# Pacing a convolution branch by counted engine work in a two-layer graph kernel, with block sums and a norm moved between engines

## The chip, the cores and the metric

The kernel runs on one core of one Trainium2 chip. A core has five engines that run their own instruction queues in order: TensorE (PE, matrix products; its weight loads appear as PEld), VectorE (DVE), ScalarE (ACT), GpSimd (POOL) and SyncE (SP, which here only issues DMA transfers). They meet through semaphores. The metric is the device time of one execution in microseconds (us), lower being better. A profile is one execution recorded by the hardware profiler.

## The reference

There are 64 graphs of N = 256 nodes with D = 256 features, `x` (64, 256, 256), and a 0/1 adjacency `adj` of the same shape. All data is fp32. With the parameters as the setup gives them, what is computed is:

```python
# layer 0
h = relu(bn1(conv1d(x^T, w1, width 1)))                  # (64, 256, 256): channels x positions
h = bn2(conv1d(h, w2, width 17, pad 8))
x_conv = relu(h + x^T)^T
s = x @ w_se.T + b_se                                    # 3 coordinates per node
A = exp(-|s_n - s_m|^2) * adj
x_nmp = A @ relu(x @ w_msg.T + b_msg)
gi = concat(x_conv, x_nmp) @ w_ih.T + b_ih
gh = x @ w_hh.T + b_hh
r, z = sigmoid(gi_r + gh_r), sigmoid(gi_z + gh_z)
g = (1 - z) * tanh(gi_n + r * gh_n) + z * x
x = layernorm(x + g)
# layer 1
h = layernorm(x) * gamma + beta
x = layernorm(x + x + relu((adj @ h) @ W_rel + b_rel + h @ W_root))
```

The output is the last `x`. No layer couples two graphs, so the graphs may be worked on in any order.

## The kernel before

A tile has 128 partitions, so one graph of 256 x 256 is two row chunks of 128, shown in the profile as 128x512. The 64 graphs are taken in `NB` = 8 blocks of `BG` = 8. The kernel has two streams of work.

**The convolution branch.** The 17-tap convolution is done for a whole block at once, because a transform over positions turns it into 47 small products with transformed filters, and eight graphs together make the transform's operands long enough. `conv(b)` is a Python generator that emits this branch for block b, one step at a time: for each pair of graphs, transposes of x on TensorE and the width-1 convolution by `w1` (L440 to L462 of the kernel before; its output goes to `HP` by ScalarE); four VectorE operations of 2048 elements that take `HP` into the big buffer `XF`; split trees on VectorE (L105, by the helper `stt`, and L362); the products (L385, `ps_k1`, `ps_k2`, `ps_k3`), whose results a function `take` brings back, one by a ScalarE copy (L400) and two by VectorE; merge trees on VectorE; the addition of x (`xb`, L546); and transposes back (L535) with a relu to `xc`. The products' filters come from DRAM in tiles of 768 KB, for which there are three buffers. A `yield` ends a step. `yield None` asks in addition that whoever drives the generator stop there, so that a result can arrive before it is used.

**The main stages.** One loop turn k carries several graphs at different stages: `gates(k)`, seven block products of a Strassen-like scheme (L656) accumulated into four PSUM banks `ps_a`, `ps_d`, `ps_b`, `ps_c`, each result added to `g` by VectorE or ScalarE, and two additions on GpSimd (L671, L683); `gates_n(k)`; `update(k)`, the gated sum on VectorE, its norm's statistics, a chain of four small GpSimd operations (L729 to L733, with a power at L730), then four normalising activations on ScalarE (L739); `transposes_h(k-1)`, `project(k-1)` and `aggregate(k-1)`, which are layer 1, its last norm again through VectorE statistics (L707, L708), four GpSimd operations and two activations (L792); and for later graphs `factors(k+2)`, `distances(k+2)`, `mask(k+2)` (the attention matrix `AT`), `passing(k+1)` (`nmp`), `messages(k+3)` (`msg`).

The Strassen-like scheme needs sums of blocks of its left operands. `sums(k, name)` makes four additions or subtractions of 128x128 (L637 to L640) for each of `x` (`xT`), `xc` and `nmp`. They run on GpSimd, except those of `xc` for the first graph of a block, which run on VectorE.

**What sets the order.** The kernel is scheduled by hand: each engine's queue holds the instructions in the order in which the program emits them. Between the main stages of a turn stand ten calls of `pump()`. A pump emits steps of `conv(b + 1)` until the emitted share of that branch's estimated cost reaches the share of pumps called so far (`done < total * at / goal`); the estimate counts VectorE's elements and a fixed weight for TensorE's steps. So block b+1's convolution lies among block b's main stages, spread over eight turns. The last block has no convolution beside it. The first block's convolution is emitted at the head, with a list `early` of first main stages between its steps.

All PSUM tiles are of one bank, eight in rotation (`bank`). `msg`, `nmp`, `AT` and `y` have two buffers, `xT` and `adj` four, `w2` three; `g`, `gn`, `h`, `hT`, `hr` and the sums' tiles have one. SyncE's queue issues the loads in the order emitted: `load(k + 3)` (`xT`, from a DRAM copy that the convolution branch writes), `load_adj(k + 2)`, `load_x(k + 1)`, the convolution's `xn` and `xb`, and the filters. ScalarE's queue issues the DRAM copy `xt` and the output.

Of the kernel before, what the change touches and what calls it, by code (L numbers as in the profile page):

```python
# [16 lines left out]
P = 128  # L17
# [14 lines left out]
RING = 10  # L32
HG = 3 * P
# [42 lines left out]

@with_exitstack
def gnn_two_layers(
# [17 lines left out]
    nc = tc.nc  # L96
    const = ctx.enter_context(tc.tile_pool(name="const", bufs=1))
# [6 lines left out]
    def stt(o, in0, s, in1, op0=ALU.mult, op1=ALU.add):  # L104
        nc.vector.scalar_tensor_tensor(o, in0, s, in1, op0=op0, op1=op1)  # L105
# [26 lines left out]
    nc.vector.memset(mhalf, -0.5)  # L132
    ones = const.tile([P, P], F32)
    nc.vector.memset(ones, 1.0)
# [7 lines left out]
    def batch_norms():  # L142
        for i in range(2):
# [3 lines left out]
            nc.vector.tensor_scalar(sh, v_, EPS, None, ALU.add)  # L147
            nc.gpsimd.tensor_tensor(sc, sh, mhalf[:, :C], ALU.pow)
            nc.vector.tensor_mul(sc, sc, g_)
            nc.vector.tensor_mul(sh, m_, sc)  # L150
            nc.vector.tensor_sub(sh, b_, sh)
# [3 lines left out]
    def along_rows(pool):  # L155

        for i, v in enumerate((bn_scale[1], bn_shift[1])):
            ps = bank("ps_row")
            for c in range(C):
                dg = pool.tile([P, P], F32, tag="dg", name="dg", bufs=4)  # L160
                nc.vector.tensor_scalar(dg, ident, v[:, c:c + 1], None, ALU.mult)
                nc.tensor.matmul(ps[:, c * P:(c + 1) * P], ones, dg, start=True, stop=True)
# [6 lines left out]
    def filters(pool):  # L169
# [18 lines left out]
        def scaled(i, starts):  # L188
# [4 lines left out]
            nc.vector.tensor_mul(  # L193
# [5 lines left out]
        def turned(ws, n):  # L199
            ps = bank("ps_tT")  # L200
            for b in range(n):
                nc.tensor.transpose(ps[:TAPS * OB, b * P:(b + 1) * P], ws[:, b].rearrange("p k o -> p (k o)"), ident)
# [11 lines left out]
        for i, (piece, starts) in enumerate(groups):  # L214
# [7 lines left out]
            for a, o in enumerate(starts):  # L222
                ps = bank("ps_w")
                nc.tensor.matmul(ps[:, :NM * OB], TT[i][:, a, :], tap_sb, start=True, stop=True)
# [67 lines left out]
    def merge(re, im, size, phis, scales, tmp, new):  # L292
# [5 lines left out]
        for base, t in ((re, t_re), (im, t_im)):  # L298
            a, b = halves(base, n, size, False), halves(base, n, size, True)
            tt = temps(t, n, h)  # L300
            if same:
                nc.vector.tensor_sub(tt, a, b)
                yield cost(n * h)
                nc.vector.tensor_add(a, a, b)
# [55 lines left out]
    def butterflies(pairs):  # L360
        for o, a, b, n, add in pairs:
            (nc.vector.tensor_add if add else nc.vector.tensor_sub)(sl(o, n), sl(a, n), sl(b, n))  # L362
# [20 lines left out]
    def product(ps, slot, w, m):  # L383
        for c in range(C):
            nc.tensor.matmul(ps, X[:, slot, c * P:(c + 1) * P], w(m, c), start=(c == 0), stop=(c == C - 1))  # L385

    def products(b, first, sums):
# [10 lines left out]
        def take():  # L398
            k1 = sl(sums, 2).rearrange("p s e -> p (s e)")
            nc.scalar.copy(k1, p1)  # L400
            nc.vector.tensor_sub(sl(re, 2).rearrange("p s e -> p (s e)"), k1, p3)  # L401
            nc.vector.tensor_add(sl(im, 2).rearrange("p s e -> p (s e)"), k1, p2)
        return take

    def last_products(b):
# [10 lines left out]
        def take():  # L416
            nc.scalar.copy(X[:, S2 + 6, :], p1[:, :D])
            nc.scalar.copy(X[:, U + 1, :], p3[:, D:])
            nc.vector.tensor_sub(X[:, U + 2, :], X[:, S2 + 6, :], p2[:, :D])
            nc.vector.tensor_add(X[:, U + 3, :], X[:, S2 + 6, :], p1[:, D:])  # L420

            nc.vector.tensor_add(X[:, U, :], p3[:, :D], bn2_row[:, 1, :])
# [597 lines left out]
```

## Time and profile before

Three runs: 2352.86, 2353.28 and 2354.74 us; the median is 2353.28 us.

| | |
|---|---|
| the profiled execution's own time | 2354.49 us |
| its span (first to last instruction) | 2352.7 us |
| TensorE (PE) busy | 2159.4 us, 92% |
| VectorE (DVE) busy | 1845.6 us, 78% |
| GpSimd (POOL) busy | 971.1 us, 41% |
| ScalarE (ACT) busy | 877.3 us, 37% |
| memory traffic | 226.76 MB, mean 96 GB/s |
| a transfer of one w2 tile (768 KB), issue to landing | 4.9 us |
| a transfer of `xT` (256 KB), issue to landing | 3.9 us |

Block times, taken between TensorE's first gate products of blocks: 188.6 us of head before the first turn, then 279.1, 280.9, 278.0, 278.6, 278.8, 280.7 and 280.2 us for seven blocks that carry a convolution, and 207.8 us for the last block with its tail.

Shares of the span are averages over parts with different limits, so the table alone doesn't say what bounds a turn. In lines that list groups, the first number after the bar is busy time in us, then the mean of one in ns, then the idle time of that engine just before, and what released it. In lines of waits, `DVE g L691 <- PE ps_c L656: 3.8, 2, 2.1` reads: VectorE's line L691, working on `g`, waited for TensorE's `ps_c`, 3.8 us in total, twice, 2.1 at most. L105 is the helper `stt` that all scalar_tensor_tensor operations go through.

### The profile page before, as it was taken

How to read it: one execution, taken by the hardware profiler on the slowest of the kernel's cores; microseconds unless marked ns; L12 is line 12 of the kernel's file. 1: busy time of each engine (PE TensorE's matmuls, PEld its weight loads, DVE VectorE, ACT ScalarE, POOL GpSimd, SP SyncE). 2: the span in 40 equal slices, each digit the busy share in tenths (PEclk: the TensorE clock that was granted, in tenths of full speed). 3: DMA queues.
4: the chain of work that ended last, by engine and by line, in shares of the span. 5: the costliest groups of instructions: out<-in, count | busy, mean ns of one | idle time of the engine just before them, and what ended most of it. 6: DMA issues, size and time to landing. Idle time of an engine off the chain costs nothing.

```text
span 2352.7 us, 25793 instructions
## 1 busy us (share of the span) xinstructions
PE 2159.4 (92%) x8390; PEld 1482.5 (63%) x8390; DVE 1845.6 (78%) x3500; ACT 877.3 (37%) x1809; POOL 971.1 (41%) x1480
## 2 busy tenths in 40 slices
PE   7878899999999999998999999999999999999997
PEld 4565576656666566665676666665666666666664
DVE  3994999759896799949998499975989679895454
ACT  4514322443235432353224432244323533235443
POOL 1003643536334452535435264353533545254442
PEclk9989999999999999999999999999999999999998
DMA  5543152223412243232332225222341214321110
GB/s 161 171 149 117 58 170 63 81 91 110 145 58 83 74 148 112 67 108 76 118 106 90 81 68 170 63 81 94 116 135 63 84 69 148 112 66 52 42 35 18
DMA packets 213939, 226.76 MB, mean 96 GB/s; under 512 B 22327, under 2 KB 205614, under 8 KB 213806
## 3 DMA queue, kind: packets, MB, share of 16 engines
q1 hardware_dynamic: 191248, 191.14, 25.9%
q10 hardware_dynamic: 22558, 33.99, 3.9%
q8 instruction: 67, 1.10, 0.2%
q14 instruction: 66, 0.54, 0.1%
HBM read 179.22 MB, written 45.88 MB: 96 GB/s over the span
## 4 chain that ended last, share of the span: by engine, by line
DVE 44%; PE 42%; issue 6%; POOL 3%; DMA 3%; ACT 2%; SPq 0%; ACTq 0%; DVEq 0%; POOLq 0%
DVE XF L105 16%; PE ps_k L385 7%; PE ps_c L656 5%; PE ps_a L656 5%; PE ps_c L456 4%; PE ps_out L764 4%; PE ps_b L656 3%; DVE XF L362 3%; PE ps_n L700 3%; DVE x L105 3%; DVE bst L707 3%; PE ps_nmp L627 3%; DVE XF L466 2%; PE ps_out L776 2%; PE ps_d L656 2%
## 5 line engine op out<-in xcount | busy, mean ns | idle before, releaser
L105 DVE SCALAR_TENSOR_TENSOR XF<-XF 128x512 f32<-128x512 f32 (+2 forms) x800 | 595.8, 773 | 6.5
L385 PE MATMUL ps_k<-w,XF 128*128 128x256 f32 x1316 | 307.9, 388 | 43.1 <-DVE g L686 21.3
L385 PEld LDWEIGHTS ps_k<-w,XF 128*128 128x128 f32 x1316 | 248.4, 192 | 98.5 <-DVE g L686 26.9
L764 PE MATMUL ps_out<-wrr,hT 128*128 128x512 f32 x512 | 256.3, 648 | 56.2 <-ACT hT L753 56.2
L729 POOL TENSOR_TENSOR q<-mv,eps 128x4 f32<-128x4 f32 x64 | 31.3, 489 | 537.5 <-DVE mv L708 293.9
L764 PEld LDWEIGHTS ps_out<-wrr,hT 128*128 128x128 f32 x512 | 103.2, 206 | 178.5 <-issue 96.6
L594 ACT ACTIVATE msg<-msg 128x512 f32<-128x512 f32 x64 | 40.4, 631 | 359.0 <-DVE msg L588 344.8
L691 DVE TENSOR_TENSOR g<-g,ps_c 128x384 f32<-128x384 f32 x64 | 35.1, 549 | 174.6 <-PE ps_c L656 174.6
L683 POOL TENSOR_TENSOR g<-g 128x384 f32<-128x384 f32 x64 | 77.7, 1214 | 228.0 <-DVE g L681 219.3
L584 PE MATMUL ps_msg<-wms,xT 128*128 128x260 f32 x512 | 134.5, 403 | 8.2 <-DVE XF L401 4.8
L362 DVE TENSOR_TENSOR XF<-XF 128x512 f32<-128x512 f32 (+3 forms) x128 | 135.0, 1080 | 1.8
L456 PE MATMUL ps_c<-xTc,w 128*128 128x512 f32 x256 | 118.1, 604 | 11.4 <-ACT xTc L448 11.4
L627 PE MATMUL ps_nmp<-AT,msg 128*128 128x256 f32 x512 | 122.9, 384 | 1.3 <-DVE AT L620 1.3
L776 PE MATMUL ps_out<-hr,adj 128*128 128x256 f32 x512 | 121.9, 380 | 0.1
L584 PEld LDWEIGHTS ps_msg<-wms,xT 128*128 128x128 f32 x512 | 94.5, 194 | 42.1 <-issue 17.0
L700 PE MATMUL ps_n<-wn,xT 128*128 128x256 f32 x512 | 121.0, 379 | 0.0
L656 PE MATMUL ps_b<-wg,nmpsum 128*128 128x384 f32 x256 | 106.0, 496 | 16.1 <-ACT g L675 14.4
L792 ACT ACTIVATE y<-y,sh,q 128x256 f32<-128x256 f32 x128 | 69.9, 594 | 134.6 <-POOL sh L789 133.9
L700 PEld LDWEIGHTS ps_n<-wn,xT 128*128 128x128 f32 x512 | 97.3, 190 | 26.9
L688 ACT ACTIVATE g<-g 128x512 f32<-128x512 f32 x64 | 40.3, 630 | 197.0 <-DVE g L686 197.0
L776 PEld LDWEIGHTS ps_out<-hr,adj 128*128 128x128 f32 x512 | 96.4, 190 | 15.9 <-ACT hr L765 1.6
L786 POOL TENSOR_SCALAR q<-mv 128x2 f32<-128x2 f32 x64 | 29.2, 457 | 186.1 <-DVE mv L708 186.1
(154 smaller groups left out, 4894.5 us busy)
## 6 DMA issues: line engine op xcount, KB each, us to landing
w<-w2m SPq DMA_DIRECT2D x105, 768.0 KB, 4.9
xn<-in_x_dram SPq DMA_DIRECT2D x32, 512.0 KB, 4.5
xt<-xTc ACTq DMA_DIRECT2D x32, 512.0 KB, 4.3
xT<-xt SPq DMA_DIRECT2D x64, 256.0 KB, 3.9
adj<-in_adjT_dram SPq DMA_DIRECT2D x64, 256.0 KB, 2.7
x<-in_x_dram SPq DMA_DIRECT2D x64, 256.0 KB, 2.8
xb<-in_x_dram SPq DMA_DIRECT2D x32, 512.0 KB, 3.7
out_dram<-y ACTq DMA_DIRECT2D x64, 256.0 KB, 2.2
```

The lines of the kernel that those rows point to most:

```text
L105: nc.vector.scalar_tensor_tensor(o, in0, s, in1, op0=op0, op1=op1)
L362: (nc.vector.tensor_add if add else nc.vector.tensor_sub)(sl(o, n), sl(a, n), sl(b, n))
L385: nc.tensor.matmul(ps, X[:, slot, c * P:(c + 1) * P], w(m, c), start=(c == 0), stop=(c == C - 1))
L456: nc.tensor.matmul(ps, w1[:, c, o * P:(o + 1) * P], xTc[:, c, :], start=(c == 0), stop=(c == C - 1))
L584: nc.tensor.matmul(ps[:, :D + 4], XT[k][:, c, m * P:(m + 1) * P], wms[:, c, :], start=(c == 0), stop=(c == C - 1))
L627: nc.tensor.matmul(ps[:, d * N:(d + 1) * N], MSG[k][:, m, d * P:(d + 1) * P], AT[k][:, m, :], start=(m == 0), stop=(m == C - 1))
L656: nc.tensor.matmul(ps[:, :w.shape[-1]], LEFT[k, name][i], w, start=start and j == 0, stop=j == 2, skip_group_check=not start)
L683: nc.gpsimd.tensor_add(g11, g11, g01)
L700: nc.tensor.matmul(ps[:, n * D:(n + 1) * D], XT[k][:, c, n * P:(n + 1) * P], wn[:, c, :], start=(c == 0), stop=(c == C - 1))
L707: nc.vector.bn_stats(st, src)
L764: nc.tensor.matmul(ps, hT[:, c, n * P:(n + 1) * P], wrr[:, c, :], start=(c == 0), stop=(c == C - 1))
L776: nc.tensor.matmul(po, ADJ[k][:, m, n * P:(n + 1) * P], hr[:, m, :], start=False, stop=(m == C - 1), skip_group_check=True)
```

## The change

1. **Pacing.** VectorE's and TensorE's calls go through wrappers (`ve`, `te`, class `Timed`) that count, at emission, an estimate of each engine's work in a `Clock`: TensorE n x 4/2400 us for a product with n columns, 0.107 for a transpose; VectorE 0.07 + 0.00105 n us. `pump()` emits convolution steps until VectorE's count is `LEAD` = 3.5 us ahead of TensorE's, or the generator yields None. Outside of pumps VectorE's count is first raised to TensorE's (`follows`). The share of an estimated cost is gone; a pump no longer has a quota.
2. **Main stages.** `load(k + 3)` moves from the middle of the turn to its start. `mask` moves from a turn's end (for k + 2) to after the second gate step of the next turn (for k + 1), and `mask(1)` goes from `early`. `messages(k + 3)` moves from after `update`'s second step to before `passing(k + 1)`. The sums of `x` move from before the loads to after `passing(k + 1)`, those of `xc` to after `project`, those of `nmp` to after `distances`. There are still ten pumps a turn, at slightly other places.
3. **Block sums.** All of `sums` runs on VectorE: 184 groups of four small operations move from GpSimd, 736 in all; the other eight groups were on VectorE already.
4. **Last norm.** In `aggregate`, the two bn_stats and two bn_aggr a graph go. The operation y = max(y, 0) + x is split in two halves, each with an accumulated row sum (`total`). GpSimd turns the sum into minus the mean; two ScalarE Square activations with that as bias accumulate the squared deviations, writing their elementwise result into `hr`, which is free by then; three GpSimd operations make scale and shift; the two final activations stay. `aggregate` has four steps instead of three, which are called from more places.

Reused names: `ve` and `te` replace `nc.vector` and `nc.tensor` in the rest of the kernel without other effect; those lines are left out here.

```diff
...
 NB = B // BG
 RING = 10
+LEAD = 3.5
 HG = 3 * P
 PI = math.pi
...
     a = th - PI / 2 if q else th
     return math.tan(a), math.cos(a), q
+class Clock:
+    def __init__(self):
+        self.pe = self.dve = 0.0
+        self.follows = True
+    def tensor(self, name, n):
+        self.pe += 0.107 if name == "transpose" else n * 4 / 2400
+    def vector(self, name, n):
+        if self.follows:
+            self.dve = max(self.dve, self.pe)
+        self.dve += 0.07 + n * 1.05e-3
+class Timed:
+    def __init__(self, engine, spend):
+        self.engine, self.spend = engine, spend
+    def __getattr__(self, name):
+        op = getattr(self.engine, name)
+        def call(o, *args, **kwargs):
+            self.spend(name, math.prod(o.shape[1:]))
+            return op(o, *args, **kwargs)
+        return call
...
 ):
     nc = tc.nc
+    clock = Clock()
+    ve, te = Timed(nc.vector, clock.vector), Timed(nc.tensor, clock.tensor)
     const = ctx.enter_context(tc.tile_pool(name="const", bufs=1))
     conv_pool = ctx.enter_context(tc.tile_pool(name="conv", bufs=2))
...
-    def blocks(src, s1, s2, s3, s4, eng):
+    def blocks(src, s1, s2, s3, s4):
         a11, a12, a21, a22 = (src[:, c, n * P:(n + 1) * P] for n in range(C) for c in range(C))
-        eng.tensor_add(s1, a21, a22)
-        eng.tensor_sub(s2, s1, a11)
-        eng.tensor_sub(s3, a11, a21)
-        eng.tensor_sub(s4, a12, s2)
+        ve.tensor_add(s1, a21, a22)
+        ve.tensor_sub(s2, s1, a11)
+        ve.tensor_sub(s3, a11, a21)
+        ve.tensor_sub(s4, a12, s2)
         return a11, a12, s4, a22, s1, s2, s3
-    def sums(k, name, eng=None):
+    def sums(k, name):
         if name == "x":
             src = XT[k]
...
             t = work.tile([P, 3, P], F32, name=name + "sum", bufs=1)
             s3 = src[:, 0, P:]
-        LEFT[k, name] = blocks(src, t[:, 0, :], t[:, 1, :], s3, t[:, 2, :], eng or nc.gpsimd)
+        LEFT[k, name] = blocks(src, t[:, 0, :], t[:, 1, :], s3, t[:, 2, :])
     def block_product(k, i, ps, start):
...
                                  skip_group_check=True)
-            nc.vector.tensor_add(y[:, n, :], po, brel)
-        yield
-        stt(y, y, 0.0, X1[k], op0=ALU.max, op1=ALU.add)
-        mv = work.tile([P, C, 2], F32, tag="mv", name="mv3", bufs=4)
+            ve.tensor_add(y[:, n, :], po, brel)
+        yield
+        total = work.tile([P, C], F32, tag="q3", name="sum3", bufs=4)
         for n in range(C):
-            stats(mv, n, y[:, n, :])
-        q = work.tile([P, C], F32, tag="q3", name="q3", bufs=4)
+            ve.scalar_tensor_tensor(y[:, n, :], y[:, n, :], 0.0, X1[k][:, n, :], op0=ALU.max, op1=ALU.add,
+                                    accum_out=total[:, n:n + 1])
+        nc.gpsimd.tensor_scalar(total, total, -1.0 / D, None, ALU.mult)
+        yield
+        var = work.tile([P, C], F32, tag="v3", name="v3", bufs=4)
+        for n in range(C):
+            nc.scalar.activation(hr[:, n, :], y[:, n, :], AF.Square, bias=total[:, n:n + 1], accum_out=var[:, n:n + 1])
         sh = work.tile([P, C], F32, tag="sh", name="sh3", bufs=4)
-        nc.gpsimd.tensor_scalar(q, mv[:, :, 1], EPS / 4, None, ALU.add)
-        nc.gpsimd.tensor_tensor(q, q, mhalf[:, :C], ALU.pow)
-        nc.gpsimd.tensor_mul(sh, mv[:, :, 0], q)
-        nc.gpsimd.tensor_scalar(sh, sh, -1.0, None, ALU.mult)
+        nc.gpsimd.tensor_scalar(var, var, 1.0 / D, EPS / 4, ALU.mult, ALU.add)
+        nc.gpsimd.tensor_tensor(var, var, mhalf[:, :C], ALU.pow)
+        nc.gpsimd.tensor_mul(sh, total, var)
         yield
         for n in range(C):
-            nc.scalar.activation(y[:, n, :], y[:, n, :], AF.Identity, bias=sh[:, n:n + 1], scale=q[:, n:n + 1])
+            nc.scalar.activation(y[:, n, :], y[:, n, :], AF.Identity, bias=sh[:, n:n + 1], scale=var[:, n:n + 1])
         nc.scalar.dma_start(out=out[k].rearrange("(c p) d -> p c d", p=P), in_=y)
         yield
...
                 nc.gpsimd.tensor_sub(w[:, i], w[:, j], w[:, l])
     early = [lambda: messages(0), lambda: messages(1), lambda: factors(0), lambda: distances(0), lambda: mask(0),
-             lambda: factors(1), lambda: distances(1), lambda: mask(1), lambda: passing(0), lambda: messages(2),
+             lambda: factors(1), lambda: distances(1), lambda: passing(0), lambda: messages(2),
              lambda: sums(0, "x"), lambda: weight_sums((6, 2, 4), (4, 4, 0)), lambda: sums(0, "nmp"),
              lambda: weight_sums((5, 2, 4), (3, 1, 5))]
...
     for f in early:
         f()
-    sums(0, "xc", nc.vector)
-    POINTS = 10
+    sums(0, "xc")
+    clock.pe = clock.dve = 0.0
     y_left = up_left = None
     for b in range(NB):
         coming = conv(b + 1) if b + 1 < NB else iter(())
-        done, at, goal = 0.0, 0, BG * POINTS - 6
         def pump():
-            nonlocal done, at
-            at += 1
-            while done < total * at / goal:
-                t = next(coming, 1e9)
-                if t is None:
-                    break
-                done += t
+            clock.follows = False
+            while clock.dve < clock.pe + LEAD and next(coming, None) is not None:
+                pass
+            clock.follows = True
         for k in range(b * BG, (b + 1) * BG):
             ga, up = gates(k), update(k)
+            load(k + 3)
             step(ga)
+            step(y_left)
             step(up_left)
+            pump()
+            step(ga)
+            if k + 1 < B:
+                mask(k + 1)
+            step(y_left)
             pump()
             step(ga)
             step(y_left)
             pump()
-            step(ga)
-            pump()
             if k + 2 < B:
                 factors(k + 2)
             step(ga)
-            if k + 1 < B:
-                sums(k + 1, "x")
-                if (k + 1) % BG:
-                    sums(k + 1, "xc")
-            load(k + 3)
             load_adj(k + 2)
             load_x(k + 1)
...
             if k > 0:
                 transposes_h(k - 1)
+            if k + 3 < B:
+                messages(k + 3)
             pump()
             if k + 1 < B:
                 passing(k + 1)
-                sums(k + 1, "nmp")
+                sums(k + 1, "x")
             step(ga)
             gates_n(k)
...
             if k > 0:
                 project(k - 1)
+            if k + 1 < B and (k + 1) % BG:
+                sums(k + 1, "xc")
             step(up)
             pump()
             if k + 2 < B:
                 distances(k + 2)
+            if k + 1 < B:
+                sums(k + 1, "nmp")
+            pump()
             step(up)
             pump()
-            if k + 3 < B:
-                messages(k + 3)
-            pump()
-            if k + 2 < B:
-                mask(k + 2)
             agg = None
             if k > 0:
                 agg = aggregate(k - 1)
-            step(agg)
             step(agg)
             pump()
...
             pass
         if b + 1 < NB:
-            sums((b + 1) * BG, "xc", nc.vector)
+            sums((b + 1) * BG, "xc")
+    step(y_left)
     step(up_left)
+    step(y_left)
     step(y_left)
     transposes_h(B - 1)
     project(B - 1)
     agg = aggregate(B - 1)
-    for _ in range(3):
+    for _ in range(4):
         step(agg)
...
```

## The prediction, made before the changed kernel was run

> **What bounds the kernel now.** I read the page's slices first. TensorE is busy 92% of the span and VectorE 78%, so an average says TensorE. The chain that ended last says otherwise:
>
> ```profile
> DVE 44%; PE 42%; issue 6%; POOL 3%; DMA 3%; ACT 2%; SPq 0%; ACTq 0%; DVEq 0%; POOLq 0%
> ```
>
> The two take turns. So I cut one block of eight graphs, a typical one of 279 to 281 us, at the instruction that begins each turn. The table of windows (microseconds; then busy time and count of TensorE, weight loads, VectorE, ScalarE, GpSimd; then clock and DMA) shows six turns of the block, its other two, and a turn of the last block, where no convolution runs:
>
> ```profile
> 1079.30:1285.00 205.70, 187.44 (x741) 131.75 (x740) 194.82 (x363) 65.34 (x136) 102.13 (x138) 0.99 0.31 100
> 1285.00:1358.30 73.30, 71.86 (x282) 46.73 (x281) 35.64 (x73) 38.45 (x74) 22.39 (x45) 1.00 0.27 90
> 2169.00:2192.90 23.90, 23.90 (x94) 16.30 (x93) 12.33 (x32) 10.15 (x21) 10.26 (x23) 1.00 0.14 45
> ```
>
> For six turns VectorE is the bound (194.82 of 205.70; 205.70 - 187.44 is TensorE idle). For two, TensorE is (71.86 of 73.30), while VectorE has 38 us free. A main turn alone is 23.9 us of TensorE. VectorE's waits in the six turns are few:
>
> ```profile
> DVE g L691 <- PE ps_c L656: 3.8, 2, 2.1
> DVE gn L703 <- PE ps_n L700: 2.3, 2, 1.2
> DVE g L686 <- POOL g L683: 0.9, 1, 0.9
> DVE gn L105 <- ACT g L692: 0.2, 1, 0.2
> ```
>
> That is 7.2 us. TensorE's waits there (to ScalarE and VectorE) cost nothing while VectorE is the bound. What VectorE's time is made of shows in the groups of the same six turns, by shape:
>
> ```profile
> L105 DVE SCALAR_TENSOR_TENSOR XF<-XF 128x512 f32<-128x512 f32 x56 | 44.6, 821 | 0.6
> L105 DVE SCALAR_TENSOR_TENSOR y<-y,x 128x512 f32<-128x512 f32 x6 | 4.2, 692 | 0.2
> L683 POOL TENSOR_TENSOR g<-g 128x384 f32<-128x384 f32 x6 | 8.0, 1328 | 24.1 <-DVE g L681 24.1
> L640 POOL TENSOR_TENSOR nmpsum<-nmp,nmpsum 128x128 f32<-128x128 f32 x6 | 5.6, 930 | 0.0
> ```
>
> The same operation on 128x512 is 692 ns in one place and 821 on average in the convolution; single ones reach 888 where GpSimd is in a two-input operation. GpSimd pays too: a sum is 930 here and 454 to 458 in the quiet last block. I fitted VectorE's pitch, start to start, where GpSimd is idle: 0.066 + 0.00104 n us (0.33 for 256 elements, 0.60 for 512, 2.20 for 2048), 0.12 more if it reads the result just before. Priced so, the six turns hold 174.3 us; the remainder is 21.3 over price while GpSimd works (12.5 beside the block sums L637 to L640, 7.2 beside L671 and L683, 1.6 beside small ones), 2.4 other excess, and 7.3 gaps: 205.3 of 205.7.
>
> [...] Here a quiet sum is 454 against VectorE's 290. [...] but starts follow each other closer:
>
> ```profile
> 1030.83 0.26 DVE L637 TENSOR_TENSOR xcsum<-xc 128x128 f32<-128x128 f32 x1
> 1031.12 0.29 DVE L638 TENSOR_TENSOR xcsum<-xcsum,xc 128x128 f32<-128x128 f32 x1
> 1031.33 0.30 DVE L639 TENSOR_TENSOR xc<-xc 128x128 f32<-128x128 f32 x1
> 1031.56 0.28 DVE L640 TENSOR_TENSOR xcsum<-xc,xcsum 128x128 f32<-128x128 f32 x1
> 1031.76 0.54 DVE L670 TENSOR_TENSOR g<-g,ps_d 128x384 f32<-128x384 f32 x1
> ```
>
> Four sums on VectorE take 1031.76 - 1030.83 = 0.93 us.
>
> **The change part by part**, per block, with the instruction order that the changed program is built with.
>
> *Sums.* Three kinds a turn move to VectorE, 18 groups of four in the six turns, less one that was there: at 0.93 us about +16, and the 12.5 us of interference beside them go. That L671 and L683 stay keeps 7.2.
>
> *Last norm.* VectorE loses bn_stats and bn_aggr twice a turn (0.446 and 0.099 us apart), 1.09, and the 128x512 y operation (0.73) becomes two of 256 with an accumulated sum (about 0.78): about -1.0 a turn. Together main work on VectorE goes from 10.9 to 12.5 us a turn. ScalarE gains two Squares of 128x256 with accumulation; no row shows them. The nearest is L739, 598 ns; lower bound that[...]. I take 0.6, since ScalarE is busy 65 of 205.7 us, hence hidden; in the tail, where nothing hides it, it counts. GpSimd's small operations are as many as before.
>
> *Pacing.* It moves convolution steps. Summed by the built order, a turn's work is (TensorE / VectorE, turns 0 to 7): before 41.4/22.0, 24/24.5, 24/21.9, 44.8/41.4, 39.6/35.1, 28.4/28.8, 24.9/23.0, 26.7/13.1; after 41.4/15.7, 24/24.7, 24/25.0, 24/21.4, 50/51.9, 38.8/39.5, 24/26.9, 27.5/16.9. Turns 1 to 6 of VectorE: 174.7 to 189.4, that is six times 1.6 plus 4.9 of convolution work brought in (three 2.2-us operations from turn 0 enter, 1.1 of xb additions leave to turn 7, the rest rounding).
>
> *Six VectorE-bound turns after:* 189.4 + 2.5 other + 7.2 + 1.6 = 200.7. The four waits above mostly go, as VectorE holds conv work ahead of each. New ones come: the take of a product at the start of turn 5, whose VectorE subtraction waits for a ScalarE copy that stands behind four normalisations (2.2 + 1.1 us after the GpSimd chain), 3.0; a ScalarE relu of msg ahead of such a copy in turns 4 and 5, 0.6 and 1.2; g at turn 4, 0.3; margin 0.5. Sum 206.3, against 205.7: nothing gained.
>
> *Two TensorE-bound turns after:* work is 41.4 + 27.5 = 68.9 against 68.1, but 73.3 were used: 5.2 is VectorE's backlog and waits of TensorE for it. With the front-loaded operations gone from turn 0, I expect 0.6 to 1.7 of waits, of which 1.2 is new (the relu of msg(k+3) holds ScalarE while xTc copies queue behind it): 69.5 to 70.6, a gain of 2.7 to 3.8.
>
> *DMA.* The same transfers. load(k+3) now stands first on SP's queue in a turn; xT lands 3.9 us after issue and is needed some 13 us later, when messages(k+3) runs. It passes the adj and x loads, which have a turn or more to spare. Weights w take 4.9 us and are fetched three tiles ahead. I price it at nothing; a late w would cost up to 4.9 once.
>
> *Mask* moves from the turn's end to after the second gate step; passing(k+1) needs it half a turn later. Free; otherwise 0.6 a turn on VectorE's lag.
>
> *Ends.* The last graph's norm has no cover: two Squares for two stats, one more GpSimd operation (0.46), hT copies behind them: +3.4; the head has its first sums on VectorE, +1.5.
>
> Sum per block -0.6 + (2.7 to 3.8) = -2.1 to -3.2; seven blocks -15 to -22, ends +4.9: -10 to -17. The profiled execution was 2354.49 us (span 2352.7), so 2337 to 2344; the median of the runs shown is 1.2 lower, 2353.28. I forecast **2340**.
>
> **Rivals.**
> *Nothing to measure (13%).* The bounded turns stay full and TensorE's two turns keep 3.1 us of waits (68.9 + 3.1 = 72.0); the gain of 1.3 less 0.6, 0.7 a block, is cancelled by the ends: 2349 to 2358. For it: the convolution's front in turn 0 (transposes, then products by w1) gives VectorE nothing to do, so that its 38 free us can't be filled and the pacing does not balance what it counts. That is the case of a change that doesn't do what it says.
>
> *Large gain (17%).* Takes don't wait, since the copy's chain starts early enough (-5.1), and two-thirds of the remaining interference goes with calmer GpSimd timing (-3): six turns 198.2, two 69.2, a block 267.4 against 279.0: seven times -11.6, ends +4.9: about 2278. For it: GpSimd loses 12 of its 14 large operations a turn; against it: L671 and L683 directly follow VectorE work, so they still run beside its next operation.
>
> *Slower (32%).* messages(k+3) now stands before passing(k+1), and msg has two buffers. The VectorE addition that writes msg(k+3) therefore waits until TensorE has read msg(k+1) in passing(k+1), which in TensorE's queue comes after the message products; ScalarE's relu waits for the addition. Behind the addition stand all of VectorE's convolution operations, behind the relu ScalarE's copies of products, and TensorE waits for those. TensorE between the two has 1.7 us of nmp products and whatever the pump puts there, up to a product of 5.2. It decides where VectorE lags TensorE by less than about 4.5 us, the wait then being the difference. By the built order I get a lag of 4.2 to 4.9 at that place. At 3 us the wait is 1.5 a turn in 42 turns, +63: 2403; at 3.5 it is +42: 2382. So this side is centred on 2390.
>
> **Numbers.** Forecast 38%, its own range 2328 to 2348; with the large gain, faster is 0.55. Within 0.2% (4.7 us, about what a measurement of this kernel tells from no change) 0.13, slower 0.32. Of the 2 in 10 left out about half lies at each end: 2288 to 2390.
>
> **What would show it.** Right: L637 to L640 on VectorE at 0.21 to 0.29 pitch; XF operations of 128x512 near 740 ns; DVE busy about 200 in the six turns, waits on ScalarE's k1 copy of 3 us once a block; two turns of 70. Wrong if: VectorE waits for TensorE at msg L588 of before (the slower case), the six turns lie off 206 by over 4, or the y chain through two more engines delays hT, and TensorE with it, every turn.

## The result: slower by 1.8%

The changed kernel's median is 2396.05 us (2393.95 to 2399.2) against 2354.01 us of the kernel before in the same series. The ratio is 1.0178 (95% interval 1.0161 to 1.0196): 42 us lost, where the forecast was 13 us gained. The profiled execution has a span of 2392.4 us, 39.7 more than before.

Cut at the same instruction of VectorE (the sum of `ps_d` into `g`) as in the prediction, the table of windows of the changed kernel shows the six turns, the other two, and a turn of the last block. The columns are as before.

```profile
1090.60:1305.00 214.40, 197.18 (x756) 139.96 (x755) 195.67 (x429) 71.32 (x159) 48.99 (x65) 0.97 0.29 95
1305.00:1376.50 71.50, 67.99 (x267) 44.86 (x266) 34.74 (x90) 41.34 (x82) 14.03 (x27) 0.95 0.28 96
2206.40:2230.30 23.90, 23.90 (x93) 16.30 (x92) 14.83 (x43) 10.99 (x25) 5.76 (x11) 1.00 0.15 45
```

The two turns improved by 1.8 us. The six turns grew from 205.70 to 214.40. VectorE's busy time there is nearly the same as before (195.67 against 194.82), so nearly all of the added time is idle time. Its waits in those six turns:

```profile
DVE g L106 <- ACT g L710: 5.4, 3, 2.6
DVE XF L106 <- ACT XF L435: 4.3, 3, 3.0
DVE g L106 <- POOL g L718: 3.0, 3, 1.3
DVE msg L106 <- PE ps_nmp L106: 2.1, 1, 2.1
DVE g L106 <- PE ps_d L106: 1.4, 2, 1.1
```

All of VectorE's operations are on L106 now, since they go through one wrapper; tiles tell them apart. L710 is the ScalarE copy of `ps_b` into `g` (L675 before), L435 the copy of a product (L400 before), L718 the GpSimd addition (L683 before). Of the five only the third stood in the list of before, with 0.9 us; the first two are 9.7 us of waiting for ScalarE. The timeline shows one wait for the `ps_b` copy. The columns are start, duration, engine, line, operation and tiles:

```profile
1402.76 0.18 DVE L106 BATCH_NORM_AGGREGATE mv<-bst 128x2 f32<-128x6 f32 x1
...
1403.02 0.20 POOL L764 TENSOR_TENSOR q<-mv,eps 128x4 f32<-128x4 f32 x1 [12.81 <-DVE mv L106]
1403.30 1.04 POOL L765 TENSOR_TENSOR q<-q,mhalf 128x4 f32<-128x4 f32 x1
1404.42 0.37 POOL L767 TENSOR_TENSOR sh<-mv,q 128x4 f32<-128x4 f32 x1
1404.88 1.09 POOL L768 TENSOR_SCALAR sh<-sh 128x4 f32<-128x4 f32 x1
...
1406.00 1.09 ACT L774 ACTIVATE h<-x,sh,q 128x256 f32<-128x256 f32 x2 [4.41 <-POOL sh L768]
1407.00 1.08 ACT L774 ACTIVATE x<-x,sh,q 128x256 f32<-128x256 f32 x2
1407.98 0.46 ACT L710 COPY g<-ps_b 128x384 f32<-128x384 f32 x1
...
1408.47 0.56 DVE L106 TENSOR_TENSOR g<-g,ps_c 128x384 f32<-128x384 f32 x1 [2.59 <-ACT g L710]
```

Read it as a loop. VectorE ends the statistics of `update(k-1)` at 1402.94. GpSimd turns them into scale and shift until 1405.97. ScalarE then runs four normalising activations. Behind them in its queue stands the copy of `ps_b` for the next graph's gates, whose product had been ready since 1402. VectorE needs the copied `g` for the sum of `ps_c`, and stands for 2.59 us, with its convolution work queued behind that sum. The least time from statistics to that sum is about 4.6 us (2.0 to 2.2 on GpSimd at its shortest, 1.98 of activations, 0.5 of copy). I measured this distance in each turn, as a mean over five blocks. In the kernel before it is 4.6 in one turn of eight, and 7 to 16 in the others. In the changed kernel it is between 4.7 and 6.1 in seven turns of eight. In four of these turns VectorE waits for the copy, and its own work in the stretch is 1.8 to 3.9 us. Three things of before no longer lie in it: the additions of `messages`, the product that `mask` makes (in this turn it starts at 1408.94, after the sum), and the last norm's statistics.

Blocks take 283.1 to 285.9 us now, 278.0 to 280.9 before: +33.6 us over seven. The head adds 4.0 (192.6 against 188.6) and the last block 2.1 (209.9 against 207.8), which sums to the 39.7.

### The profile page after: what moved, and what is told of

Its sections match the earlier page's. It is cut to its first block, busy times and chain, and to the rows that moved or that the text cites. A ratio compares the mean times of both kernels' runs of the same rounds, so it can differ in the third digit from the quotient of the medians.

```text
span 2392.4 us, 26243 instructions
## 1 busy us (share of the span) xinstructions
PE 2173.5 (91%) x8390; PEld 1508.2 (63%) x8390; DVE 1869.8 (78%) x4172; ACT 946.0 (40%) x2065; POOL 506.9 (21%) x744
## 5 line engine op out<-in xcount | busy, mean ns | idle before, releaser
L106 DVE SCALAR_TENSOR_TENSOR XF<-XF 128x512 f32<-128x512 f32 (+2 forms) x800 | 521.9, 688 | 6.8
L106 DVE TENSOR_TENSOR XF<-XF 128x256 f32<-128x256 f32 (+3 forms) x480 | 357.5, 764 | 43.9 <-ACT XF L494 36.3
L106 PE MATMUL ps_k<-w,XF 128*128 128x256 f32 x1316 | 295.1, 380 | 2.9 <-DVE msg L106 1.5
L106 PEld LDWEIGHTS ps_k<-w,XF 128*128 128x128 f32 x1316 | 250.8, 191 | 51.4 <-issue 4.3
L106 PE MATMUL ps_out<-wrr,hT 128*128 128x512 f32 x512 | 232.2, 596 | 4.6 <-ACT hT L788 4.6
L106 PE MATMUL ps_b<-wg,nmpsum 128*128 128x384 f32 x256 | 115.5, 535 | 107.7 <-ACT g L710 85.5
L106 PEld LDWEIGHTS ps_out<-wrr,hT 128*128 128x128 f32 x512 | 97.4, 192 | 103.4 <-issue 89.2
L106 PE MATMUL ps_nmp<-AT,msg 128*128 128x256 f32 x512 | 130.5, 400 | 25.2 <-DVE g L106 22.5
L774 ACT ACTIVATE h<-x,sh,q 128x256 f32<-128x256 f32 x128 | 69.8, 593 | 200.9 <-POOL sh L768 200.9
L631 POOL TENSOR_SCALAR st<-ns 128x4 f32<-128x4 f32 x64 | 25.4, 397 | 580.8 <-DVE sq L106 357.8
L106 DVE TENSOR_TENSOR g<-g,ps_c 128x384 f32<-128x384 f32 x128 | 70.4, 550 | 90.6 <-ACT g L710 63.9
L106 PE MATMUL ps_msg<-wms,xT 128*128 128x260 f32 x512 | 127.8, 393 | 3.9 <-DMA adj<-in_adjT_dram 3.5
L106 PEld LDWEIGHTS ps_b<-wg,nmpsum 128*128 128x128 f32 x256 | 44.2, 198 | 137.6 <-ACT g L710 93.6
L106 PE MATMUL ps_out<-hr,adj 128*128 128x256 f32 x512 | 128.1, 392 | 1.0 <-ACT hr L800 0.9
L106 PEld LDWEIGHTS ps_nmp<-AT,msg 128*128 128x128 f32 x512 | 99.8, 199 | 43.4 <-DVE g L106 25.4
L106 PE MATMUL ps_c<-xTc,w 128*128 128x512 f32 x256 | 118.2, 604 | 8.6 <-ACT xTc L483 8.6
L718 POOL TENSOR_TENSOR g<-g 128x384 f32<-128x384 f32 x64 | 84.5, 1320 | 183.9 <-DVE g L106 183.2
L106 DVE TENSOR_TENSOR msg<-ps_msg,bmsg 128x256 f32<-128x256 f32 x128 | 52.5, 416 | 88.7 <-PE ps_nmp L106 88.7
L106 PE MATMUL ps_n<-wn,xT 128*128 128x256 f32 x512 | 120.9, 379 | 0.0
L106 PE MATMUL ps_c<-wg,nmp 128*128 128x384 f32 x256 | 110.0, 513 | 9.1 <-DVE y L106 9.1
L831 ACT ACTIVATE y<-y,sh,v 128x256 f32<-128x256 f32 x128 | 69.9, 593 | 121.1 <-POOL sh L828 118.3
```

What stands on the lines that cost most here:

```text
L106: return op(o, *args, **kwargs)
L631: nc.gpsimd.tensor_scalar(twice[:, :, :, 3], ns.unsqueeze(2).to_broadcast([P, C, 2]), 0.5, None, ALU.mult)
L718: nc.gpsimd.tensor_add(g11, g11, g01)
L774: nc.scalar.activation(dst[:, n, :], w[:, n, :], AF.Identity, bias=sh[:, i, n:n + 1], scale=q[:, i, n:n + 1])
L831: nc.scalar.activation(y[:, n, :], y[:, n, :], AF.Identity, bias=sh[:, n:n + 1], scale=var[:, n:n + 1])
```

## Experiments

Three theories were on the table. N: the loop through ScalarE's queue is the cause. V: VectorE is full in the six turns, and waits are only where slack shows. M: the prediction's slower rival, two buffers of `msg`. Edits are to the changed kernel unless said otherwise. "Six" and "two" are the two kinds of turns, mean of five blocks (before 206.5 and 72.8, changed 213.7 and 70.4), "idle" is VectorE's idle time in the six, in gaps of over 0.1 us (before 8.1, changed 14.5). I call the loop open in a kernel where VectorE no longer waits for the `ps_b` copy in the six turns, closed where it does as in the changed kernel.

### The copy ahead of the activations

```diff
             step(y_left)
-            step(up_left)
             pump()
             step(ga)
+            step(up_left)
             if k + 1 < B:
                 mask(k + 1)
```

> The four normalising activations of update(k-1) are emitted after the second gate step instead of before it, so ScalarE's copy of ps_b, and at the start of a turn the copy of a product, stand ahead of them. Theory N (those copies wait behind activations that wait for the GpSimd chain, and VectorE waits for the copies: in a block 8.3 us at the ps_b copy and 4.3 us at the product's copy): the two waits fall below 2 us a block, a block from 284 to 272-276, the time to 2312-2340 us. Theory V (the six turns are full of VectorE work, 199 us of it, and a wait only shows where slack is): the waits turn up elsewhere, 2386-2396 us. Theory M (msg waits for nmp): unchanged, 2396 us.

Measured: 2340.34 us, 0.9945 of before (0.9928 to 0.9962). Six 205.4, idle 5.7, two 71.5. One block's six turns of this kernel, in the view of VectorE's waits:

```profile
DVE g L106 <- POOL g L718: 3.0, 3, 1.2
DVE XF L106 <- ACT XF L435: 1.3, 2, 1.1
DVE g L106 <- PE ps_d L106: 1.1, 1, 1.1
DVE msg L106 <- PE ps_nmp L106: 0.4, 1, 0.4
```

The wait for the `ps_b` copy is gone, the product's copy waits 1.3 instead of 4.3, and 56 us come back. No work was removed. By the traces TensorE, VectorE and GpSimd run the changed kernel's instructions in its order; only ScalarE's order differs. N holds, V falls: in the six turns no other wait took their place. In the two turns one did: TensorE's wait for the `ps_b` copy (3.4 us a block) goes, and one of 3.2 us for a ScalarE copy of `lr` comes (`PE ps_xc <- ACT lr`), and these turns take 71.5, not less than 70.4.

### The messages late, and both edits

```diff
-            if k + 3 < B:
-                messages(k + 3)
             pump()
             if k + 1 < B:
                 passing(k + 1)
...
             step(up)
             pump()
+            if k + 3 < B:
+                messages(k + 3)
             agg = None
```

> messages(k+3) goes back behind update's second step, where it stood before, so the addition into msg finds passing(k+1) done. Theory M: VectorE's wait for nmp (10.2 us a block, 6.7 of them in the turn that TensorE bounds and so free) goes, 3.5 us a block, 2371 us. Theory N: the message additions also come between the statistics and the ps_b copy and cover about 1 us of each of four waits, so 2360-2375 us, with the wait for the ps_b copy still 4 us a block. Theory V: 2391-2401 us.

> Both edits at once, activations after the ps_b copy and messages late; each alone had brought the changed kernel to 2340 and 2338 us. Theory N (one loop: statistics on VectorE, GpSimd chain, four activations, ps_b copy, and VectorE's next use of it; either edit opens it): nothing left to gain twice, only what is over of waits in the six turns (product copy 1.3, nmp 1.0 us), 2325-2340 us. Theory of two separate causes: the two gains of 56 us add, 2285-2300 us.

Measured: 2338.41 us (0.9931, 0.9915 to 0.9947) for the messages alone, 2339.51 (0.9937, 0.9918 to 0.9956) for both. The first gained more than any theory gave it: the `ps_b` wait did not shrink, it vanished. TensorE's message products and VectorE's additions now lie between the statistics and the sum of `ps_c`, which come 5.5 us or more apart in every turn. This edit also takes away the wait that M names, and the order on every engine shifts with it, so it is the less clean test of the two. Two edits worth 56 and 58 us alone are worth 57 together. They open the same loop. What is left differs: with the messages late the six turns are 208.2 with idle 7.7, of which 3.3 is a new wait for `ps_d`, and the two turns are 68.5.

### Three buffers of msg

```diff
-        MSG[k] = work.tile([P, C, D], F32, tag="msg", name="msg")
+        MSG[k] = work.tile([P, C, D], F32, tag="msg", name="msg", bufs=3)
...
-        y = work.tile([P, C, D], F32, tag="y", name="y")
+        y = work.tile([P, C, D], F32, tag="y", name="y", bufs=1)
```

> The changed kernel with three buffers of msg (y has one instead of two to make room), so that the addition into msg(k+3) has no wait for passing(k+1); the order is the changed kernel's. The rival of the prediction (two buffers of msg hold VectorE): the wait for nmp, 1.6 us a block in the six turns and 9.4 in the two, goes. If it is also what sets off the waits for the ps_b copy: 2338-2350 us. If it is only its own 1.6 us a block: 2380-2390 us. Theory N: the waits for the ps_b copy stay at 5 us in the six turns, 2380-2396 us.

Measured: 2380.62 us (1.0109, 1.0092 to 1.0126). VectorE's waits in six turns:

```profile
DVE g L106 <- ACT g L710: 5.4, 3, 2.6
DVE XF L106 <- ACT XF L435: 4.2, 3, 3.0
DVE g L106 <- POOL g L718: 3.0, 3, 1.3
DVE g L106 <- PE ps_d L106: 1.1, 1, 1.1
```

The wait for `ps_nmp` is gone as built, the two waits for ScalarE stand within a tenth. (Every engine runs the changed kernel's instructions in its order.) So the rival's mechanism exists and costs 15 us, and is not what the other waits come from.

### Two of four activations ahead of the copy

```diff
             for n in range(C):
                 nc.scalar.activation(dst[:, n, :], ...)
+            if i:
+                yield
...
             step(ga)
+            step(up_left)
             if k + 1 < B:
                 mask(k + 1)
...
```

> Only two of the four normalising activations (those of h) stand ahead of the ps_b copy, the other two follow it. Theory N: each of the four waits of a block shortens by two activations, 1.1 us: the wait for the ps_b copy in the six turns from 5.4 to about 2.2 us a block, for the product's copy from 4.3 to 3.2, in all -5.5 us a block with the seventh turn, 2355-2362 us. Theory of a wait that is set by something else than the activations: 2390-2396 us.

Measured: 2361.36 us (1.0029, 1.0021 to 1.0037). The `ps_b` wait is 2.6 (2.2 expected), the product's copy 3.3 (3.2 expected). Four activations ahead: 2396; two: 2361; none: 2340. The order on the other engines is again the same. The wait follows the length of what stands ahead of the copy.

### A longer lead, with the loop closed and open

```diff
-LEAD = 3.5
+LEAD = 6.0
```

> The pacing's lead is 6.0 us instead of 3.5. Theory N: VectorE holds 2.5 us more of convolution work ahead of each of the four waits of 2 to 3 us for the ps_b copy, which shrink to below 1 us: 2340-2365 us. Theory V: the same VectorE work in the six turns, only earlier, 2390-2400 us. Theory M: a larger lag of VectorE hides its wait for nmp in the six turns, 1.5 us a block, 2385 us.

> The first experiment's order (activations after the ps_b copy) with a lead of 6.0 us. Theory N says that the longer lead hurt the changed kernel (2411 us) because VectorE reaches the norm's statistics later while TensorE's b product is no later, so that five of eight turns, not four, waited on the loop. With the loop open the lead has nothing to hurt: 2330-2345 us. If a longer lead costs by itself, by late product results or full buffers: 2350-2360 us.

Measured: 2411.3 us (1.0239, 1.0219 to 1.026) in the changed kernel, 2333.75 (0.9916, 0.989 to 0.9943) with the copy ahead of the activations. The first refutes my expectation: I had thought that more convolution work queued on VectorE would cover the wait. It is queued in front of the statistics too, so the loop starts later: measured from the end of the `ps_b` product, the statistics end 0.8 to 7.9 us later than in the changed kernel in four of eight turns. Six turns of eight stand at 5.2 us or less, and the `ps_b` wait doubles to 10.3 us. With the loop open the same lead does no harm.

### Block sums back on GpSimd, or moved alone

```diff
-        LEFT[k, name] = blocks(src, t[:, 0, :], t[:, 1, :], s3, t[:, 2, :])
+        LEFT[k, name] = blocks(src, t[:, 0, :], t[:, 1, :], s3, t[:, 2, :], eng or nc.gpsimd)
```

(`blocks` calls its four operations on `eng` again.) In the changed order, then with the copy ahead of the activations; third, the kernel before with `eng` always VectorE:

> All of the change but the block sums, which go back to GpSimd at their new places. Theory V: VectorE's work in six turns falls by 16 us, interference beside the sums returns with 12, and the copies wait as before, but VectorE is no longer full: 2360-2380 us. Theory N: the waits for the copies stay, and a sum's four operations on GpSimd (3 us) are now ahead of the GpSimd chain of the norm, so that it starts later: 2396-2420 us. Theory M: 2396 us.

> The first experiment's order with all block sums back on GpSimd. With the loop open, the prediction's term for the sums stands alone: -15.8 us of VectorE's work and +12.5 of interference in the six turns, -3 us a block: 2315-2335 us. If the sums on GpSimd delay what waits for GpSimd (the norm's chain, the additions to g), or their products: 2345-2365 us.

> The kernel before with nothing changed but the block sums, all on VectorE. By the prediction's sum: in the six turns +15.8 us of work and -12.5 of interference, +3.3 us a block less what was idle there, so 2354-2378 us. If the interference beside the sums costs more than the sums do on VectorE: 2330-2350 us. If VectorE is full and interference is not freed: up to 2460 us.

Measured: 2417.21 us (1.0268, 1.025 to 1.0286); 2339.04 (0.9934, 0.9915 to 0.9954); 2376.51 (1.009, 1.007 to 1.011). In the kernel before, moving the sums costs 21 us: six turns 209.2, +2.7, where the prediction's sum had +3.3. VectorE's time without idle grew by more, 6.8 (the sums take 16.8, and 10.0 of other operations' time goes); idle fell from 8.1 to 3.9. In the open loop it is worth nothing (2339 against 2340), which lies between the two expectations. In the closed loop GpSimd sums make all worse, with idle 28.8 (the `ps_b` copy 8.1, `msg` 4.5, the GpSimd addition 3.8). In two turns the norm's activations start 1.2 and 1.9 us later after the statistics, in another VectorE has 3.0 us less to do while it waits. What each of these costs was not taken apart.

### The last norm, three times

The norm's statistics back on VectorE (`bn_stats`, `bn_aggr`), no Squares: with the copy ahead, then in the changed kernel; third, the kernel before with only the new norm.

```diff
-        total = work.tile([P, C], F32, tag="q3", name="sum3", bufs=4)
-        for n in range(C):
-            ve.scalar_tensor_tensor(y[:, n, :], ..., accum_out=total[:, n:n + 1])
...
+        stt(y, y, 0.0, X1[k], op0=ALU.max, op1=ALU.add)
+        mv = work.tile([P, C, 2], F32, tag="mv", name="mv3", bufs=4)
+        for n in range(C):
+            stats(mv, n, y[:, n, :])
```

> The first experiment's order with the last norm's statistics back on VectorE (bn_stats), without the Squares on ScalarE. By the prediction's term, VectorE has 1.0 us more in each turn, 6 us in the six turns that it bounds, and seven blocks: +42 less what the tail wins back (3), so 2370-2380 us. If ScalarE's Squares cost as much as they free: 2335-2345 us.

> The changed kernel, its loop as it is, with only the last norm's statistics back on VectorE. Theory N: the two bn_stats and bn_aggr add 1.1 us of VectorE work a turn between update's statistics and the use of the ps_b copy, which is inside the loop, where VectorE was waiting anyway: each wait shortens by 1.1 us as in the experiment with two of four activations, and with what the norm gave in the open loop (-23 us) 2335-2355 us. The prediction's term alone (+1.0 us a turn on a full VectorE): 2430-2438 us. If only the open loop gained: about 2396 us.

> The kernel before with only the new last norm, Squares on ScalarE. The prediction's term: VectorE 1.1 us less a turn, 6.6 in the six turns, seven blocks, tail +3: 2310-2330 us. Theory N: VectorE's work saved lies inside the loop of statistics, activations and ps_b copy only where the loop is tight (in the kernel before one turn of eight is at its least time), so a gain of part of that: 2325-2345 us. If the Squares cost on ScalarE what they free, as the open-loop runs hint: 2355-2380 us.

Measured: 2316.94 us (0.9843, 0.9826 to 0.9861); 2340.89 (0.9955, 0.994 to 0.997); 2316.15 (0.9851, 0.983 to 0.9871). Six turns of the last one, which is the kernel before with one part of the change:

```profile
1063.90:1264.30 200.40, 185.38 (x741) 131.78 (x742) 187.61 (x356) 70.29 (x158) 101.21 (x138) 1.00 0.33 104
```

VectorE is busy 7.2 us less than before (187.61 against 194.82) and the six turns are 5.3 us shorter (200.40 against 205.70). The same part in the changed order is a loss of 55 us (2396 against 2341). There the last norm's statistics lie between the loop's start and end. Taking 1.1 us of them away gave VectorE nothing to do earlier; it only waited longer. With them back, one block's six turns have

```profile
DVE XF L106 <- ACT XF L435: 1.7, 2, 1.1
DVE g L106 <- ACT g L710: 1.5, 3, 0.6
```

in place of 4.3 and 5.4.

That the open loop too runs 23 us faster with the old norm I had not expected: by the prediction's term it should have lost, to 2370 to 2380. VectorE pays the 6.0 us in the six turns that the sum says; of it come back 3.7 in convolution operations (two fewer fall into the six turns), 0.9 in the mask and 1.6 of idle time, so the six turns stay at 205, and the two turns shorten from 71.5 to 68.3, with less waiting for `ps_nmp`. The pacing places steps differently, as its count gives a `bn_stats` of six results 0.08 us where the trace has 0.45. That this is why is argued, not shown.

### The old pump in the new order

```diff
             clock.follows = False
-            while clock.dve < clock.pe + LEAD and next(coming, None) is not None:
-                pass
+            nonlocal done, at
+            at += 1
+            while done < total * at / goal:
+                ...
```

Made with the copy ahead of the activations.

> The first experiment's order of main stages, sums and norm with the old pump, which follows the share of an estimated cost. If the count is what makes the order work: VectorE's backlog returns into the two turns that TensorE bounds (+3 us a block) against 4.9 us less convolution work in the six turns that VectorE bounds, and waits where the quota leaves VectorE without work (7 us a block in the kernel before): 2345-2375 us. If the pacing is worth nothing: 2335-2345 us. If the quota is better with the loop open: 2315-2333 us.

Measured: 2366.41 us (1.0048, 1.003 to 1.0067), 26 us slower than with the count. Six turns have idle 10.8, of which 8.9 is VectorE's `msg` waiting for `ps_nmp`. So the prediction's slower rival costs most here, where the quota, as I read it, leaves VectorE too little work just ahead of that addition.

### The two GpSimd additions to g on VectorE

```diff
-        nc.gpsimd.tensor_add(g00, g00, bg[:, 1, :])
+        ve.tensor_add(g00, g00, bg[:, 1, :])
...
-        nc.gpsimd.tensor_add(g11, g11, g01)
+        ve.tensor_add(g11, g11, g01)
```

Made in the 2317 us kernel (copy ahead, old norm).

> The fastest kernel so far (2317 us: activations after the copy, norm's statistics on VectorE) with the two additions to g moved from GpSimd to VectorE. VectorE gains 2 x 0.47 us a turn, 5.6 in the six turns; of interference beside these two up to 7.2 us and of waits for the GpSimd addition 2.9 us go, all in all -4.5 us a block: 2285-2300 us. If the remaining excess of VectorE isn't interference: 2330-2345 us.

Measured: 2411.55 us (1.0253, 1.0232 to 1.0274), a clear miss. VectorE's time without idle in the six turns went from 200.9 to 201.7 only, though 5.9 us of additions came in. That is not interference gone. Eight of the convolution's operations left the six turns for the two, as one block of each kernel shows (the 2317 us kernel first):

```profile
L106 DVE SCALAR_TENSOR_TENSOR XF<-XF 128x512 f32<-128x512 f32 x55 | 36.7, 701 | 0.5
L106 DVE SCALAR_TENSOR_TENSOR XF<-XF 128x512 f32<-128x512 f32 x47 | 30.7, 685 | 0.5
```

The eight account for some 5.5 us. Those that stayed became only 16 ns shorter each, 0.8 us in all, where up to 7.2 us of interference was expected to go. Idle rose from 4.1 to 11.5 (`msg` for `ps_nmp` 5.0, product's copy 4.6), and the two turns, where VectorE's work grew by 6.7 us, from 68.3 to 74.2. The pump's counts shift with every operation moved, and with them where products and trees land. Which shift did it is open.

## Why the prediction was wrong, and where it was right

*VectorE's work in the six turns: right.* 200.7 us without waits were forecast, 199.2 measured (mean of five blocks). Interference beside the sums went: the convolution's 128x512 operations, 821 ns before and "near 740" forecast, are

```profile
L106 DVE SCALAR_TENSOR_TENSOR XF<-XF 128x512 f32<-128x512 f32 x56 | 38.2, 715 | 0.6
L824 ACT ACTIVATE hr<-y,sum 128x256 f32<-128x256 f32 x12 | 6.0, 503 | 1.7 <-POOL sum L820 1.7
```

The second line is the Square, 0.50 us apart, where 0.6 was taken. Single terms of the sum were off. No group of sums stood on VectorE in these six turns before, so 18 came, not 17; and three additions of `xb` left them, not one. The terms of single parts, tested on the kernel before, held in time: the sums +2.7 a block against +3.3, the new norm -37 us in all against -1.0 x 42 + 3 = -39. In part that is luck, since VectorE's work moved by more (+6.8 and -8.1 in the six turns) and its idle time took up the difference (3.9 and 10.3, for 8.1 before).

*The two turns: the number right, by luck.* They take 70.4, against 69.5 to 70.6. The forecast was 68.9 of TensorE's work and 0.6 to 1.7 of waits. TensorE is busy 66.0 there and waits 4.3 (mean of five blocks), most of it in this line (one block):

```profile
PE ps_b L106 <- ACT g L710: 3.0, 1, 3.0
```

It is the `ps_b` copy again, for which TensorE waits as well.

*The waits: wrong, and this is the step that failed.* "The four waits above mostly go, as VectorE holds conv work ahead of each. New ones come", with 5.6 us in all. The measured sum is 14.5 (mean of five blocks): the `ps_b` copy 5.4 and the GpSimd addition 3.0 were not in it, unless the 0.3 for `g` in one turn stood for the latter; the product's copy was 4.3 instead of 3.0, and `msg`, which the forecast left to its slower rival, 1.6. The chain of the four normalisations behind the GpSimd operations was named, but only for a product's copy at the start of one turn. The `ps_b` copy stands behind the same four activations in every turn. I took VectorE's queued work to cover it, and did not subtract, turn by turn, the VectorE work between statistics and use from the 4.6 us that the loop needs at least. In the changed order, where `messages`, the mask and the last norm's statistics no longer lie between, that work is less than the loop in four turns of eight. Either the messages or the statistics put back end most of the waiting for the copy (2338 and 2341 us); the mask alone was not tried. With the loop open (the copy ahead) the waits are 5.7 and the time is 2340.34, the forecast's 2340. That it meets the forecast so closely is chance: the six turns are 205.4 against 206.3, the two 71.5 against 69.5 to 70.6.

*The ends:* +4.0 at the head against +1.5, +2.1 at the tail against +3.4, of little weight.

*The slower rival: the number right, the mechanism mostly not.* It gave 2382 to 2403 by `msg` waiting for `passing`. That wait is 1.6 us in six turns, and a third buffer wins 15 us of 56. The larger part is the loop. A time that lies in a rival's band does not prove the rival.

*The large gain* needed the product's copy not to wait; it waited more.

*What the change is worth by parts* depends on what it is combined with: the new norm alone gains 37 us in the old order and loses 55 in the new one; the count gains 26 us over the quota in the new order with the loop open; the sums cost 21 us in the old order and nothing in the open new one. Fastest were the kernel before with the new norm (2316 us) and the changed kernel with the copy ahead and the old norm (2317 us). The first with the copy moved as well was not tried.

## What to carry to other kernels

Where queues run in order, write down every loop that leaves an engine and returns to it (here VectorE, GpSimd, ScalarE, VectorE), its least time, and the returning engine's own work between the two ends; when stages are moved, recompute that difference in each turn before counting any work saved. Work saved inside such a loop turned into waiting here (1.1 us a turn of the last norm's statistics, a loss of 55 us in the changed order), and queued work in front of its start made it worse (a lead of 6.0 instead of 3.5 us, 15 us more). In a queue, an operation whose input is ready (here the copy of `ps_b`, worth 56 us) belongs ahead of those that still wait for another engine.

## What the runs showed of the hardware

TensorE's busy time rose from 2159.4 to 2173.5 us with the same 8390 matmuls, and the mean granted clock fell from 0.976 to 0.962; with the loop open it is 0.975. The table of windows over a few us of the changed kernel, in a turn where VectorE's sums of `nmp` are late, shows a stretch at half clock (start and end, length, then busy time of TensorE, its weight loads, VectorE, ScalarE, GpSimd; third from the end the clock):

```profile
1504.60:1506.60 2.00, 1.57 (x6) 0.76 (x4) 1.93 (x7) 0.00 (x0) 0.00 (x0) 1.00 0.00 0
1506.60:1508.60 2.00, 0.00 (x0) 0.00 (x0) 1.97 (x4) 0.00 (x0) 0.00 (x0) 1.00 0.00 0
1508.60:1510.60 2.00, 1.78 (x5) 1.22 (x6) 1.93 (x6) 0.00 (x0) 0.00 (x0) 0.82 0.00 0
1510.60:1512.60 2.00, 0.93 (x2) 0.00 (x0) 1.86 (x7) 0.48 (x1) 0.00 (x0) 0.50 0.00 0
1512.60:1514.60 2.00, 1.56 (x3) 0.95 (x4) 1.87 (x8) 0.00 (x0) 1.61 (x3) 0.50 0.04 8
1514.60:1516.60 2.00, 2.00 (x5) 1.23 (x4) 0.00 (x0) 1.73 (x4) 1.38 (x3) 0.50 0.00 0
1516.60:1518.60 2.00, 2.00 (x10) 1.76 (x9) 1.16 (x2) 2.00 (x7) 0.00 (x0) 0.97 0.00 0
```

TensorE waits 2.7 us, works on, and then has half the clock for 6.83 us (1509.89 to 1516.72), with another wait of 1.5 us in them. In the changed kernel's clock records 32 of 36 stretches of half clock last 3.41 or 6.83 us. Not every wait of this kind was followed by such a stretch: after its first 300 us the changed kernel has 20 waits of TensorE of 2.5 to 3.0 us, and 11 were followed by half the clock within 5 us of their start. The one of 2.8 us in the turn that the timeline above shows was not. What decides it was not shown. In all, half clock was granted for 185 us of the changed kernel and 117 us of the kernel before. In such a stretch the same products take longer: the two of `ps_b` with `xcsum` took 1.49 us at 1510.04, against 0.81 at 1401.18 in the turn of the timeline. So where half clock follows a wait of TensorE, the products after it take longer too.

In the sixth window VectorE stands idle, but not for TensorE. It waits for ScalarE's copy of a product that TensorE had finished at 1500.2. This copy stands behind the four activations (the second line of VectorE's waits):

```profile
1517.44 1.28 DVE L106 TENSOR_TENSOR XF<-XF,ps_k 128x512 f32<-128x512 f32 x2 [2.97 <-ACT XF L435]
```

What the lower clock cost the changed kernel, no run isolated; a part of the 56 us may be this.
